# A graph-network layer on one core: selected columns in two of five groups, raw input rows for the first four groups, a later store of the node features

## The chip, the cores and the metric

The kernel runs on one core of a Trainium2 chip. The metric is device time in microseconds (us) of one execution; the time before is the median of three. A core has TensorE (PE; its weight loads are PEld), VectorE (DVE), ScalarE (ACT), GpSimd (POOL) and SyncE (SP, which here only issues transfers), and 16 DMA engines that all queues share. SBUF is the memory the engines work in, PSUM the one that TensorE writes to.

## The reference, cut to what matters

There are 12500 nodes with 64 features and 412500 edges, sorted by receiver (`dst`), each with 32 features.

```python
h = jnp.maximum(_layernorm(x, axis=-1), 0.0)
msg_in = concat([h[src], h[dst], edge_attr_32])         # 64 + 64 + 32
messages = swish(msg_in @ W1 + b1) @ W2 + b2
att = softmax(swish(msg_in @ Wa1 + ba1) @ Wa2 + ba2, axis=0)   # over all edges
aggregated = segment_sum(messages * att, dst)
out = x + swish(concat([h, aggregated]) @ Wu1 + bu1) @ Wu2 + bu2
```

## The kernel before, in words

`[h[src], h[dst], e] @ [Wa1, W1]` is a sum of three terms, and the first two depend on a node alone. So the kernel first makes two tables of 128 columns with a row for each node: `ts_d` (as sender) and `tr_d` (as receiver, with the biases).

**Node stage** (`gnn_kernel`, L164 to L312). x is read in eight chunks (L174, SyncE). For each chunk VectorE and ScalarE normalize: a sum (L219), the mean subtracted (L221), Square (L227), a sum (L232), Sqrt (L235), reciprocal (L240), ReLU and product (L242). TensorE transposes (L254), and ScalarE copies the result into `hT` (L256), which stays in SBUF as 128 x 6272: two nodes' 64 features above each other. From `hT` TensorE makes the rows of `ts_d` (L269, copied at L271, stored at L273) and of `tr_d` (L305, L307, stored at L309 from ScalarE's queue). Then `hT` itself is stored to `hT_d` (L312, same queue). Only `general`, a second way through that runs when the edges' order doesn't suit the first, reads `hT_d`.

**Edge stage** (`one_pass`). Edges are taken in 413 groups of 8 x 125. In iteration g of the main loop (L735) these are issued, each engine keeping the written order (`pin`):

- `begin(g)` (L567): VectorE adds the group's PSUM sum `pe` to its gathered rows `gs` (L570); ScalarE takes Tanh (L573; swish is computed from it).
- pieces of `sum_up` for earlier groups (L711): the softmax weights, TensorE's sum by receiver (L637, L643), the projection (L654), and the addition into `sums` (L668, L672).
- for g < 4 ScalarE fills a quarter of `sums` and of `stand` (L749).
- `burst(g, 0)`, then `load(g + 2)`, `numbers(g + 7)`, `places(g + 6)`, `end(g)`, `burst(g, 1)`.

`load(g)` (L523) takes one of seven `gs` buffers (L161). GpSimd issues the indirect gathers, one for each 125 edges, out of `ts_d` (L530). SyncE loads the edge features `eo` (L541) and receiver numbers `dbs` (L544) for four groups at a time and two windows of `tr_d` (`wins`, L551). VectorE compares (L555), and TensorE adds receiver and edge terms in `pe` (L559). GpSimd runs ahead of the other engines as far as `gs` buffers are free. `end(g)` (L575) reads `gs` for the last time in L583 and L589 on VectorE; L591 and L594 follow.

**Chosen groups** gather 7 times for 8. The last 125 rows are computed instead: SyncE loads their sender numbers (`numbers`, L477), six small VectorE instructions turn them into places in `hT` (`places`, L486 to L492), ScalarE loads the places into registers and copies 125 single columns of `hT` (`columns`, L503) in lots spread over three earlier iterations (`burst`, `SLOTS`), VectorE masks the half that isn't meant (L564), and TensorE multiplies with the stacked weights into `pe` (L565). `begin` then has a copy (L572) for the eighth. Before the change, every third group from 8 to 400 is chosen, 131 of them, in six lots of at most 24 columns.

`load(0)` and `load(1)` stand ahead of the loop, behind the setup of `one_pass` (L420 to L469 on VectorE), whose tiles lie where the node stage's were.

The last part (L799 on) turns `sums` into the output; its length does not depend on the change.

Of the kernel before, what the change touches and what calls it, by code (L numbers as in the profile page):

```python
# [44 lines left out]
F32 = mybir.dt.float32  # L45
I32 = mybir.dt.int32
AF = mybir.ActivationFunctionType
ALU = mybir.AluOpType
AX = mybir.AxisListType
# [4 lines left out]
P = 128  # L54
EP = 125
D = 64
DE = 32
U = 64
C = 2 * U
S1 = U + 1  # L60
K = 8
# [5 lines left out]
H = K // 2  # L67
# [3 lines left out]
NC = 8  # L71
TABLES = 4

EVERY = 3
PHASE = 1
SLOTS = (((0, 24), (24, 24)), ((48, 24), (72, 12)), ((84, 24), (108, 17)))
ROUND = 12582912.0
EPS = 1e-5
NEG = -3.0e38
BIG = 3.0e38  # L80
# [9 lines left out]
def gnn_kernel(ctx: ExitStack, tc: tile.TileContext, n_edges, x, src, src_row, dst, dst_row, first, edge,  # L90
               weights, out):
    nc = tc.nc
    NB = x.shape[0] // P
    T = src.shape[1]
    NG = T // K
# [4 lines left out]
    const = ctx.enter_context(tc.tile_pool(name="const", bufs=1))  # L100
# [4 lines left out]
    hT_d = dram.tile([2 * D, NB // 2, P], F32, name="hT_d")  # L105
# [6 lines left out]
    ident = const.tile([P, P], F32, name="ident")  # L112
# [9 lines left out]
    w_pair = part["pair"].rearrange("p (r n) -> p r n", r=2)  # L122
    wu2h = part["wu2h"].rearrange("p (h d) -> p h d", h=2)
    we, bias, wa2, bu2_r, ba2_c = (part[k] for k in ("we", "bias", "wa2", "bu2", "ba2"))
# [30 lines left out]
    hT = const.tile([2 * D, NB // 2, P], F32, name="hT")  # L155
# [5 lines left out]
    gather = ctx.enter_context(tc.tile_pool(name="gather", bufs=7))  # L161


    with tc.tile_pool(name="node1", bufs=1) as node1, \  # L164
            tc.tile_pool(name="node", bufs=2) as node, \
            tc.tile_pool(name="node_ps", bufs=2, space=PSUM) as node_ps:
# [36 lines left out]
            pin(nc.vector.tensor_tensor(fall, base_p[:, :NG - 1], base_p[:, 1:], ALU.subtract))  # L203
            pin(nc.vector.tensor_reduce(far[:, 2:3], fall, AX.X, ALU.max))

        eps = node1.tile([P, 1], F32, name="eps")
        nc.vector.memset(eps, EPS)
        pin(nc.scalar.activation(node1.tile([P, 1], F32, name="spare"), eps, AF.Sqrt))
        xms, sqs, rstds, hs, tss = ({} for _ in range(5))
# [99 lines left out]
            pin(nc.scalar.dma_start(  # L309
                tr_d[:NP, :].rearrange("(p b) f -> p b f", b=NB)[:, c:c + nn, :], tr))  # L310
        pin(nc.scalar.dma_start(tr_d[NP:, :], zero[:WR, :]))
        pin(nc.scalar.dma_start(hT_d, hT))  # L312

    one_pass(tc, n_edges, locals())
    again = nc.values_load(wrong[0:1, 0:1], min_val=0, max_val=1,
# [77 lines left out]
def one_pass(tc, n_edges, v):  # L393
    nc = tc.nc
# [16 lines left out]
    with ExitStack() as ctx:  # L411
# [43 lines left out]
        with tc.tile_pool(name="work2", bufs=2) as work2, \  # L455
# [12 lines left out]
            for h in range(2):  # L468
                nc.vector.tensor_copy(w2u[:, h, :], w2u_ps)  # L469

            chosen = {g for g in range(8, NG - 12) if g % EVERY == PHASE}

            def numbers(g):
                if g in chosen:
                    e = (g * K + K - 1) * EP
                    n = nums[g] = small.tile([P, EP], I32, name="num", bufs=2)
                    nc.sync.dma_start(n, bass.AP(tensor=v["src_row"].tensor,  # L477
                                                 offset=v["src_row"][:, e:].offset, ap=[[0, P], [1, EP]]))

            def places(g):  # L480
                if g not in chosen:
                    return
                n = nums[g]
                near = small.tile([1, EP], F32, name="near", bufs=1)
                to = small.tile([1, EP], I32, name="to", bufs=2)
                pin(nc.vector.tensor_scalar(to, n[0:1], 1, None, op0=ALU.logical_shift_right))  # L486
                m = NB // 2
                pin(nc.vector.tensor_scalar(near, to, 1.0 / m, 0.5 / m - 0.5, op0=ALU.mult, op1=ALU.add))
                pin(nc.vector.tensor_scalar(near, near, ROUND, None, op0=ALU.add))
                pin(nc.vector.tensor_scalar(near, near, ROUND, float(1 - m * P), op0=ALU.subtract, op1=ALU.mult))  # L490
                pin(nc.vector.scalar_tensor_tensor(to, to, float(P), near, op0=ALU.mult, op1=ALU.add))
                pin(nc.vector.tensor_scalar(n, n, 1, None, op0=ALU.bitwise_and))  # L492
                cols[g] = small.tile([P, EP], F32, name="cols", bufs=2), to

            def columns(g, first, n):
                if g not in chosen:
                    return
                to, at = cols[g]
                _, regs = nc.values_load_multi_w_load_instructions(
                    at[0:1, first:first + n], engines=[ENG.Activation], min_val=0, max_val=NP // 2 - 1,  # L500
                    skip_runtime_bounds_check_because=WHY)
                for i in range(n):
                    pin(nc.scalar.copy(to[:, first + i:first + i + 1], hT[:, bass.ds(regs[i], 1)]))  # L503

            def burst(g, k):
                for i in range(EVERY):
                    columns(g + 3 + i, *SLOTS[EVERY - 1 - i][k])

            at_sp, at_lo, at_hi, bus, rest = {}, {}, {}, {}, {}

# [4 lines left out]
            def registers(g, engine, at, base=base_sb, top=NP - 1):  # L515
# [4 lines left out]
                for i in range(n):  # L520
                    at[g + i] = regs[i]

            def load(g):  # L523

                t = g * K
                if g % NQ == 0:
                    registers(g, ENG.SP, at_sp)
                gs = gss[g] = gather.tile([P, K, C], F32, name="gs")[:EP]
                for j in range(K - (g in chosen)):
                    nc.gpsimd.indirect_dma_start(  # L530
                        out=gs[:, j, :], out_offset=None, in_=ts_d[:, :],
                        in_offset=bass.IndirectOffsetOnAxis(ap=src_sb[:, t + j:t + j + 1], axis=0))
                if g % NQ == 0:
                    n = min(NQ, NG - g) * E2
                    eo = eos[g // NQ % 2]
                    i = g // NQ % 2
                    db = dbs[i * WR:(i + 1) * WR].bitcast(I32)
                    for i in range(g, min(g + NQ, NG)):
                        e = slice((i - g) * E2, (i - g + 1) * E2)
                        ees[i] = eo[:, e], db[:, e]  # L540
                    nc.sync.dma_start(eo[WR:, :n],  # L541
                                      edge[:, g * E2:g * E2 + n])
                    for r in range(2):
                        nc.sync.dma_start(  # L544
                            db[r * R:(r + 1) * R, :n],
                            bass.AP(tensor=dst_row.tensor, offset=dst_row[r:r + 1, g * E2:].offset,
                                    ap=[[0, R], [1, n]]))
                eo, db = ees.pop(g)
                win = wins[g % WINS]
                for r in range(2):  # L550
                    nc.sync.dma_start(win[r * R:(r + 1) * R, :, r, :],  # L551
                                      tr_w[bass.ds(at_sp[g], R), :, :])
                for h in range(2):
                    e = slice(h * E2 // 2, (h + 1) * E2 // 2)
                    pin(nc.vector.tensor_scalar(eo[:WR, e], db[:, e], bj[g // NQ % 2 * WR:(g // NQ % 2 + 1) * WR, g, h:h + 1], None,  # L555
                                                op0=ALU.is_equal))
                pe = pes[g] = pre_ps.tile([P, K, C], F32, name="pe")[:EP]
                for q in range(H):
                    pin(nc.tensor.matmul(pe[:, 2 * q:2 * q + 2, :], eo[:, q * EP:(q + 1) * EP],  # L559
                                         win[:, q // 2, :, :], start=True,  # L560
                                         stop=q < H - 1 or g not in chosen))
                if g in chosen:
                    to, _ = cols[g]
                    pin(nc.vector.scalar_tensor_tensor(to, nums[g], half, to, op0=ALU.is_equal, op1=ALU.mult))  # L564
                    pin(nc.tensor.matmul(pe[:, K - 1, :], to, stack, start=False, stop=True))  # L565

            def begin(g):  # L567

                n = K - (g in chosen)
                pin(nc.vector.tensor_tensor(gss[g][:, :n, :], pes[g][:, :n, :], gss[g][:, :n, :], ALU.add))  # L570
                if n < K:
                    pin(nc.vector.tensor_copy(gss[g][:, n, :], pes[g][:, n, :]))  # L572
                pin(nc.scalar.activation(pes[g], gss[g], AF.Tanh))  # L573
# [111 lines left out]
            def inputs(t):  # L685

                n = P // 2 * NC
                if t < 8:
                    i = (t // 4 + (NG - 1) // NQ + 1) % 2
                    bs[t], xs[t] = eos[i][:, t % 4 * n:(t % 4 + 1) * n], hT[:, t * n:(t + 1) * n]  # L690
                else:
                    gs = gather.tile([P, K, C], F32, name="gs").rearrange("p k c -> p (k c)")
                    bs[t], xs[t] = gs[:, :n], gs[:, n:]
                m = width(t)
                bs[t], xs[t] = bs[t][:, :P // 2 * m], xs[t][:, :m * D]
                nc.sync.dma_start(bs[t], bq_d[t, :, :P // 2 * m])
                nc.sync.dma_start(xs[t], xb_d[t, :, :m * D])
# [37 lines left out]
            for g in range(NG):  # L735
# [38 lines left out]
                        weigh_upto(batch[g])  # L774
                for t in {NG - 5: [0, 1], NG - 4: [2, 3], NG - 2: range(4, NT)}.get(g, []):
                    inputs(t)
                if g == min(30, NG):
                    pin(nc.vector.tensor_reduce(far[:, 0:1], dloc, AX.X, ALU.max))
                    pin(nc.vector.tensor_scalar(far[:, 0:1], far[:, 0:1], -float(R - 1), None,
                                                op0=ALU.add))  # L780
# [357 lines left out]
```

## Time and profile before

| | |
|---|---|
| median of 3 runs | 4922.53 us (4922.45 to 4923.75) |
| the profiled execution | 4935.06 us, span 4933.3 us |
| mean granted TensorE clock | 0.611 |
| gathers (L530) | 3173, of 125 rows of 512 B |
| column copies (L503) | 16375 |
| traffic | HBM read 361.41 MB, written 25.72 MB; 78 GB/s over the span |
| GpSimd's queue | 206.77 MB, 19.0% of the 16 DMA engines |
| the store `hT_d<-hT` | 1 transfer of 3136.0 KB |

The profiled execution takes slightly longer than the others, and the durations below are from it. A busy share is of the whole span. A group of instructions has its line, engine, operation, output and inputs, and count, then its busy time and the mean of one, then the idle time of its engine just ahead of it and what ended it; "issue" means that nothing the profile shows was waited for. A timeline line has start, duration, engine and line; in brackets stands the idle time ahead of it. A transfer's line on a queue is the issue, not its landing.

### The profile page before, as it was taken

Reading aid. Unit: us, or ns where it says so; the run is one execution under the profiler, and the core shown is the slowest. Engines: PE = TensorE matmul, PEld = TensorE weight load, DVE = VectorE, ACT = ScalarE, POOL = GpSimd, SP = SyncE. Lnnn points to the kernel's source line nnn. Section 1 sums busy time; section 2 is a strip of 40 time slices with the busy share of each in tenths; the row PEclk is TensorE's granted clock in tenths of the full one; section 3 lists DMA queues with packets and bytes.
Section 4 is the critical chain, followed back from the end, with each engine's and each line's share of the span. In section 5 each row is a group of like instructions: output and inputs, shape, how many; then the busy total and the mean of one; then the engine's idle time right before and its main releaser. Section 6 shows DMA issues by size and latency. Waiting matters only on the chain. (4 is left out here: it accounts for less than half of the span.)

```text
span 4933.3 us, 81829 instructions
## 1 busy us (share of the span) xinstructions
PE 2429.9 (49%) x11509; PEld 1950.7 (40%) x11509; DVE 3456.5 (70%) x9793; ACT 2214.0 (45%) x17625; POOL 3871.1 (78%) x3198
## 2 busy tenths in 40 slices
PE   5455555445544444544444544444445445444455
PEld 4343344334433333433333443333334334334344
DVE  6677777777776766766766776766767667667667
ACT  3444444444444444444444444444444444444412
POOL 4777877777777777777777777777777777777775
PEclk8666655665666665555665555566566666655655
DMA  7333333333333333333333333233333333333333
GB/s 248 76 76 83 87 75 82 89 74 83 81 75 76 71 74 76 70 75 76 69 76 76 68 76 76 68 76 76 69 76 71 74 76 70 75 76 70 75 91 81
DMA packets 377225, 396.20 MB, mean 80 GB/s; under 512 B 230333, under 2 KB 306039, under 8 KB 376290
## 3 DMA queue, kind: packets, MB, share of 16 engines
q0 software_dynamic: 253840, 206.77, 19.0%
q1 hardware_dynamic: 121458, 174.49, 14.9%
q10 hardware_dynamic: 1376, 9.67, 0.5%
q14 instruction: 457, 3.74, 0.3%
q8 instruction: 94, 1.54, 0.1%
HBM read 361.41 MB, written 25.72 MB: 78 GB/s over the span
## 5 line engine op out<-in xcount | busy, mean ns | idle before, releaser
L530 POOL DMA_INDIRECT gs<-ts_d,src_sb x3173 | 3853.9, 1215 | 1020.6 <-issue 962.4
L559 PE MATMUL pe<-wins,eo 128*125 128x256 f32 x3304 | 1524.4, 637 | 1551.2 <-DVE eo L555 1288.7
L503 ACT COPY cols<-hT 128x1 f32 x16375 | 1630.2, 189 | 754.3 <-issue 749.8
L559 PEld LDWEIGHTS pe<-wins,eo 128*125 128x125 f32 x3304 | 997.4, 319 | 1872.4 <-DVE eo L555 1375.5
L570 DVE TENSOR_TENSOR gs<-pe,gs 125x1024 f32<-125x1024 f32 (+1 forms) x413 | 487.5, 1180 | 1153.1 <-DMA gs<-ts_d,src_sb 1140.2
L573 ACT ACTIVATE pe<-gs 125x1024 f32<-125x1024 f32 x413 | 424.8, 1029 | 1768.2 <-DVE gs L570 859.2
L637 DVE TENSOR_SCALAR wt<-iota_w,dloc,p 125x40 f32<-125x40 f32 x3304 | 772.5, 364 | 1.8
L643 PE MATMUL sp<-wt,acts 125*65 125x40 f32 x6608 | 652.2, 270 | 13.2 <-DVE wt L637 9.2
L643 PEld LDWEIGHTS sp<-wt,acts 125*65 125x65 f32 x6608 | 612.5, 185 | 23.6 <-DVE wt L637 14.0
L613 PE MATMUL mt<-ident,mx 125*128 125x125 f32 x110 | 48.1, 438 | 644.7 <-DVE sums L672 608.1
L654 PEld LDWEIGHTS mt<-ss,w2u 65*128 65x128 f32 x826 | 210.7, 283 | 362.0 <-issue 235.4
L654 PE MATMUL mt<-ss,w2u 65*128 65x40 f32 x826 | 188.3, 322 | 262.8 <-DVE gm L620 199.4
L555 DVE TENSOR_SCALAR eo<-dbs,bj 64x250 f32<-64x250 int32 x826 | 303.2, 397 | 17.9 <-DMA dbs<-in_dst_row_dram 8.5
L591 DVE TENSOR_TENSOR pe<-pe,w_all 125x512 f32<-125x512 f32 x413 | 288.8, 699 | 13.7
L589 DVE SCALAR_TENSOR_TENSOR pe<-pe,gs 125x512 f32<-125x512 f32 x413 | 287.4, 696 | 10.8
L583 DVE SCALAR_TENSOR_TENSOR acts<-pe,gs 125x512 f32<-125x512 f32 x413 | 284.6, 689 | 12.8 <-issue 2.4
L594 DVE TENSOR_REDUCE lg<-pe 125x8 f32<-125x512 f32 x413 | 284.2, 688 | 10.8
L613 PEld LDWEIGHTS mt<-ident,mx 125*128 125x128 f32 x110 | 20.0, 182 | 655.8 <-issue 652.2
L675 DVE COPY stand<-nmax 64x40 f32 x826 | 217.1, 263 | 3.3
L672 DVE TENSOR_TENSOR sums<-sums,mt 64x40 f32 x606 | 114.4, 189 | 4.7 <-issue 0.4
L668 DVE SCALAR_TENSOR_TENSOR sums<-sums,scale,mt 64x40 f32 x220 | 55.8, 254 | 78.4 <-PE mt L654 59.6
L356 DVE TENSOR_SCALAR bu<-mt,w_all 64x256 f32<-64x256 f32 (+1 forms) x50 | 23.9, 478 | 92.6 <-PE mt L347 78.6
(124 smaller groups left out, 1123.2 us busy)
## 6 DMA issues: line engine op xcount, KB each, us to landing
eo<-in_edge_dram SPq DMA_DIRECT2D x103, 500.0 KB
dbs<-in_dst_row_dram SPq DMA_DIRECT2D x206, 250.0 KB
gs<-ts_d,src_sb POOLq DMA_INDIRECT x3173
wins<-tr_d SPq DMA_DIRECT2D x826, 32.0 KB
num<-in_src_row_dram SPq DMA_DIRECT2D x131, 62.5 KB
ts_d<-ts SPq DMA_DIRECT2D x5, 896.0 KB
tr_d<-tr ACTq DMA_DIRECT2D x5, 896.0 KB
hT_d<-hT ACTq DMA_DIRECT2D x1, 3136.0 KB
```

Of the source, the lines that this page charges most:

```text
L503: pin(nc.scalar.copy(to[:, first + i:first + i + 1], hT[:, bass.ds(regs[i], 1)]))
L530: nc.gpsimd.indirect_dma_start(out=gs[:, j, :], out_offset=None, in_=ts_d[:, :], in_offset=bass.IndirectOffsetOnAxis(ap=src_sb[:, t + j:t ...
L555: pin(nc.vector.tensor_scalar(eo[:WR, e], db[:, e], bj[g // NQ % 2 * WR:(g // NQ % 2 + 1) * WR, g, h:h + 1], None, op0=ALU.is_equal))
L559: pin(nc.tensor.matmul(pe[:, 2 * q:2 * q + 2, :], eo[:, q * EP:(q + 1) * EP], win[:, q // 2, :, :], start=True, stop=q < H - 1 or g not in ...
L570: pin(nc.vector.tensor_tensor(gss[g][:, :n, :], pes[g][:, :n, :], gss[g][:, :n, :], ALU.add))
L573: pin(nc.scalar.activation(pes[g], gss[g], AF.Tanh))
L583: pin(nc.vector.scalar_tensor_tensor(acts[g % ACTS][:, :, 0:U], th[:, :, U:C], 1.0, gs[:, :, U:C], op0=ALU.add, op1=ALU.mult))
L589: pin(nc.vector.scalar_tensor_tensor(att, th[:, :, 0:U], 1.0, gs[:, :, 0:U], op0=ALU.add, op1=ALU.mult))
L591: pin(nc.vector.tensor_tensor(att, att, wa2[:EP, None, :].to_broadcast([EP, K, U]), ALU.mult))
L637: pin(nc.vector.tensor_scalar(wt[:, j, :], iota_w[:EP, j // H, :], dloc[:, g * K + j:g * K + j + 1], p[:, k + j:k + j + 1], op0=ALU.is_equ ...
L643: pin(nc.tensor.matmul(sp, acts[g % ACTS][:, j, :], wt[:, j, :], start=j == 0, stop=j == K - 1))
L654: pin(nc.tensor.matmul(pp, w2u.rearrange("s h u -> s (h u)"), sps.pop(g), start=True, stop=True))
```

## The change

- **Columns.** Chosen are groups whose number modulo 5 is 1 or 4, again from 8 to 400. A group's 125 columns come in five lots (four of 24, one of 29), so that each iteration's two bursts have one lot each. The tiles `num`, `to` and `cols` get three buffers for two.
- **First four groups.** At the kernel's start, four `gs` buffers are filled by 32 gathers out of the input x itself (rows of 64 numbers), whose indices have a small load of their own. In place of the gathers out of `ts_d`, `load(g)` for g < 4 calls `features(g)`: it normalizes the rows on the edges (VectorE and ScalarE), transposes them (TensorE) and copies them back (ScalarE); a second product in `load` adds the sender's term to `pe`, and `begin` copies `pe` instead of adding.
- **Store of hT.** The one store from ScalarE's queue at the end of the node stage becomes seven from SyncE's, in iterations 20 to 26.

```diff
-EVERY = 3
-PHASE = 1
-SLOTS = (((0, 24), (24, 24)), ((48, 24), (72, 12)), ((84, 24), (108, 17)))
+LOTS = ((0, 24), (24, 24), (48, 24), (72, 24), (96, EP - 96))
+ROUNDS = 5
+SLOTS = {1: ((5, 1), (4, 0), (4, 1), (3, 0), (3, 1)), 4: ((5, 0), (5, 1), (4, 0), (4, 1), (3, 0))}
+RAW = 4
...
     gather = ctx.enter_context(tc.tile_pool(name="gather", bufs=7))
+    raw_src = const.tile([P, RAW * K], I32, name="raw_src")
+    nc.scalar.dma_start(raw_src, src[:, :RAW * K])
+    raws = [gather.tile([P, K, C], F32, name="gs") for _ in range(RAW)]
+    for g in range(RAW):
+        for j in range(K):
+            nc.gpsimd.indirect_dma_start(
+                out=raws[g].rearrange("p k c -> p (k c)")[:EP, j * D:(j + 1) * D], out_offset=None, in_=x[:, :],
+                in_offset=bass.IndirectOffsetOnAxis(ap=raw_src[:EP, g * K + j:g * K + j + 1], axis=0))
...
-        pin(nc.scalar.dma_start(hT_d, hT))
...
-            chosen = {g for g in range(8, NG - 12) if g % EVERY == PHASE}
+            chosen = {g for g in range(8, NG - 12) if g % ROUNDS in SLOTS}
...
             def burst(g, k):
-                for i in range(EVERY):
-                    columns(g + 3 + i, *SLOTS[EVERY - 1 - i][k])
+                for i in (3, 4, 5):
+                    slots = SLOTS.get((g + i) % ROUNDS, ())
+                    if (i, k) in slots:
+                        columns(g + i, *LOTS[slots.index((i, k))])
...
+            def features(g):
+                gs = gss[g] = v["raws"][g][:EP]
+                xg, xm = (gs[:, h * H:(h + 1) * H, :].rearrange("p k (r d) -> p (k r) d", d=D) for h in range(2))
+                total = small.tile([EP, K], F32, name="raw_t", bufs=1)
+                pin(nc.vector.tensor_reduce(total, xg, AX.X, ALU.add))
+                pin(nc.vector.scalar_tensor_tensor(xm, total[:, :, None].to_broadcast([EP, K, D]), -1.0 / D, xg,
+                                                   op0=ALU.mult, op1=ALU.add))
+                pin(nc.scalar.activation(xg, xm, AF.Square))
+                rstd = small.tile([EP, K], F32, name="raw_r", bufs=1)
+                pin(nc.vector.tensor_reduce(rstd, xg, AX.X, ALU.add))
+                pin(nc.scalar.activation(rstd, rstd, AF.Sqrt, bias=v["eps"][:EP], scale=1.0 / D))
+                pin(nc.vector.reciprocal(rstd, rstd))
+                pin(nc.vector.scalar_tensor_tensor(xg, xm, 0.0, rstd[:, :, None].to_broadcast([EP, K, D]),
+                                                   op0=ALU.max, op1=ALU.mult))
+                pt = one_ps.tile([P, 4, P], F32, name="mt")[:, :, :EP]
+                for q in range(H):
+                    pin(nc.tensor.transpose(pt[:, q, :], xg[:, 2 * q:2 * q + 2, :], ident[:EP, :EP]))
+                to = raw_to[g] = v["raws"][g][:, H:, :EP]
+                pin(nc.scalar.copy(to, pt))
...
-                gs = gss[g] = gather.tile([P, K, C], F32, name="gs")[:EP]
-                for j in range(K - (g in chosen)):
+                if g < RAW:
+                    features(g)
+                else:
+                    gss[g] = gather.tile([P, K, C], F32, name="gs")[:EP]
+                gs = gss[g]
+                for j in range(0 if g < RAW else K - (g in chosen)):
...
                     pin(nc.tensor.matmul(pe[:, 2 * q:2 * q + 2, :], eo[:, q * EP:(q + 1) * EP],
                                          win[:, q // 2, :, :], start=True,
-                                         stop=q < H - 1 or g not in chosen))
+                                         stop=g >= RAW and (q < H - 1 or g not in chosen)))
+                    if g < RAW:
+                        pin(nc.tensor.matmul(pe[:, 2 * q:2 * q + 2, :], raw_to[g][:, q, :], v["w_pair"][:, 0],
+                                             start=False, stop=True))
...
-                pin(nc.vector.tensor_tensor(gss[g][:, :n, :], pes[g][:, :n, :], gss[g][:, :n, :], ALU.add))
+                if g < RAW:
+                    pin(nc.vector.tensor_copy(gss[g], pes[g]))
+                else:
+                    pin(nc.vector.tensor_tensor(gss[g][:, :n, :], pes[g][:, :n, :], gss[g][:, :n, :], ALU.add))
...
+                if 20 <= g < 27:
+                    n = -(-(NB // 2) // 7)
+                    q = slice((g - 20) * n, min((g - 19) * n, NB // 2))
+                    nc.sync.dma_start(v["hT_d"][:, q, :], v["hT"][:, q, :])
```

More of the change, by code (lines that the diff above doesn't have):

```diff
@@ L204, in windows @@
             pin(nc.vector.tensor_reduce(far[:, 2:3], fall, AX.X, ALU.max))
-        eps = node1.tile([P, 1], F32, name="eps")
+        eps = const.tile([P, 1], F32, name="eps")
         nc.vector.memset(eps, EPS)
@@ L475, in numbers @@
                     e = (g * K + K - 1) * EP
-                    n = nums[g] = small.tile([P, EP], I32, name="num", bufs=2)
+                    n = nums[g] = small.tile([P, EP], I32, name="num", bufs=3)
                     nc.sync.dma_start(n, bass.AP(tensor=v["src_row"].tensor,
@@ L484, in places @@
                 near = small.tile([1, EP], F32, name="near", bufs=1)
-                to = small.tile([1, EP], I32, name="to", bufs=2)
+                to = small.tile([1, EP], I32, name="to", bufs=3)
                 pin(nc.vector.tensor_scalar(to, n[0:1], 1, None, op0=ALU.logical_shift_right))
@@ L492, in places @@
                 pin(nc.vector.tensor_scalar(n, n, 1, None, op0=ALU.bitwise_and))
-                cols[g] = small.tile([P, EP], F32, name="cols", bufs=2), to
+                cols[g] = small.tile([P, EP], F32, name="cols", bufs=3), to
             def columns(g, first, n):
@@ L521, in registers @@
                     at[g + i] = regs[i]
+            def features(g):
[17 more added lines that the diff above has]
+                pin(nc.scalar.copy(to, pt))
+            raw_to = {}
             def load(g):
```

## The prediction

> **What bounds the kernel now.** I read the busy table and the costliest groups first, then GpSimd's own timeline from end to end, then the other engines around its first gathers, and last one iteration of the loop.
>
> The groups of the page (line, engine, operation, count; then busy us, mean ns; then idle time ahead and what ended it):
>
> ```profile
> PE 2429.9 (49%) x11509; PEld 1950.7 (40%) x11509; DVE 3456.5 (70%) x9793; ACT 2214.0 (45%) x17625; POOL 3871.1 (78%) x3198
> ...
> L530 POOL DMA_INDIRECT gs<-ts_d,src_sb x3173 | 3853.9, 1215 | 1020.6 <-issue 962.4
> ...
> L503 ACT COPY cols<-hT 128x1 f32 x16375 | 1630.2, 189 | 754.3 <-issue 749.8
> L570 DVE TENSOR_TENSOR gs<-pe,gs 125x1024 f32<-125x1024 f32 (+1 forms) x413 | 487.5, 1180 | 1153.1 <-DMA gs<-ts_d,src_sb 1140.2
> L573 ACT ACTIVATE pe<-gs 125x1024 f32<-125x1024 f32 x413 | 424.8, 1029 | 1768.2 <-DVE gs L570 859.2
> ```
>
> GpSimd (POOL) does nothing but 3173 gathers, and its idle time is "issue": it waits for no one. VectorE (DVE) waits 1140.2 us for gathers, 2.76 us in each of 413 groups, and ScalarE (ACT) waits for VectorE. GpSimd's timeline shows where the row starts and how it runs:
>
> ```profile
> 51.89 1.38 POOL L530 DMA_INDIRECT gs<-ts_d,src_sb  x1 [49.48 <-issue]
> 53.57 1.21 POOL L530 DMA_INDIRECT gs<-ts_d,src_sb  x1 [0.31 <-issue]
> ...
> 140.77 1.21 POOL L530 DMA_INDIRECT gs<-ts_d,src_sb  x1 [0.30 <-issue]
> ...
> 152.90 1.21 POOL L530 DMA_INDIRECT gs<-ts_d,src_sb  x1 [0.30 <-issue]
> ```
>
> Before 51.89 GpSimd is empty for 49.48 us, because the gathered table ts_d must be stored first. Group 7's first gather (the 57th) starts at 140.77, group 8's (the 65th) at 152.90, the last at 4875.68. From group 8 to the last are 3108 steps: 4722.8 / 3108 = **1.5196 us a gather**, with no gap worth naming. The end behind the last gather, some 57 us, is not touched by the change. So two things count: how many gathers there are from group 8 on, and when group 8's first one starts.
>
> **Part 1: columns.** Chosen groups are those from 8 to 400: with one in three 131, with two in five 78 + 79 = 157. Each saves a gather: 26 x 1.5196 = **39.5 us**. What it adds lies on engines that wait:
> - ScalarE: 26 x 125 = 3250 column copies. The first row below gives 24 in 2.32 us, 0.097 each: 315 us, 0.8 us for each of 393 groups. Register loads stay (785 lots of columns for 786). Waits before the tanh hide it (3.76 us in the second row).
> - VectorE: L486 to L492 take 1.75 us, L564 0.35, L572 0.28: 2.38 x 26 = 62 us, 0.16 a group, hidden in its 2.76. Without cover it would cost those 62.
> - TensorE: 52 more passes at L565 of 376 ns, 20 us, at 49% busy. SyncE: 26 loads of 62.5 KB; its own waits are for TensorE at L551, so nothing queues behind them that is late.
>
> ```profile
> 1014.16 2.32 ACT L503 COPY cols<-hT 128x1 f32 x24 [1.49 <-issue]
> ...
> 1020.65 1.03 ACT L573 ACTIVATE pe<-gs 125x1024 f32<-125x1024 f32 x1 [3.76 <-DVE gs L570]
> ```
>
> One row speaks against it. The gather that starts at 122.44, beside L486 to L490, took 1.33 us for 1.21:
>
> ```profile
> 122.44 1.33 POOL L530 DMA_INDIRECT gs<-ts_d,src_sb  x1 [0.30 <-issue]
> ```
>
> All that the 3173 gathers take beyond 1.21 (those over 1.22) sums to 9.9 us; laid wholly on 131 chosen groups it is 0.075 each, 2 us for 26. I take 0, range 0 to 2 (fewer gathers than now can't lock it less than not at all). The Trainium skill's page "SBUF — State Buffer", section "Who interferes with whom", says that VectorE's copy and tensor_scalar can take two ports and then block GpSimd for the whole instruction. By that rule the five tensor_scalar of `places` (1.46 us) could cost 26 x 1.46 = 38 us and leave almost nothing of this part; the trace shows a twentieth of it.
>
> **Part 2: the first four groups.** Their 32 gathers go to the front, where GpSimd was empty. Their indices are a small load like the first x chunk's, which VectorE used at 3.72; 32 x 1.52 from there ends at 52.3. A 256 B row may cost half (27.8) or as much as the slowest early one (1.38 + 0.30: 57.5); neither matters below. Their DMA work, at the queue's 19.0% x 4933 / 3173 = 0.295 us of all 16 engines each, is 9.5 us at most, and the engines are 71% busy in the first 52 us, so the node stage slips by 0 to 9.5. A full stretch (74 to 85) gave this queue 8.0%, so about 1 us in the full ten (10 to 20); I take **1**. Then groups 4, 5, 6: 24 gathers from 52.9 end at **89.4**.
>
> Now a new wait: there are seven buffers, four hold raw rows, so group 7 waits for the end of group 0's work, and everything on GpSimd waits behind it. When is that? Before, it stood thus:
>
> ```profile
> 74.05 1.12 ACTq L312 DMA_DIRECT2D hT_d<-hT  x1
> 77.09 0.59 SPq L541 DMA_DIRECT2D eo<-in_edge_dram  x1
> ...
> 87.98 1.21 POOL L530 DMA_INDIRECT gs<-ts_d,src_sb  x1 [1.19 <-DMA gs<-ts_d,src_sb]
> 91.82 1.21 POOL L530 DMA_INDIRECT gs<-ts_d,src_sb  x1 [2.63 <-DMA gs<-ts_d,src_sb]
> ...
> 92.93 1.12 DVE L555 TENSOR_SCALAR eo<-dbs,bj 64x250 f32<-64x250 int32 x4 [8.55 <-DMA dbs<-in_dst_row_dram]
> ...
> 94.45 7.40 PE L559 MATMUL pe<-wins,eo 128*125 128x256 f32 x24 [23.84 <-DMA wins<-tr_d]
> ...
> 98.23 1.22 DVE L570 TENSOR_TENSOR gs<-pe,gs 125x1024 f32<-125x1024 f32 x1 [4.18 <-PE pe L559]
> ...
> 99.52 1.28 ACT L573 ACT_TABLE_LOAD   x1 [51.29 <-DMA eo<-in_edge_dram]
> ```
>
> The 3136 KB store of hT lies ahead of the loads that group 0 needs. With it gone, 1.0 MB of eo and dbs at 272 GB/s takes some 4 us from 77.7, and wins, issued at 82.2, is there by about 86. That no longer is last. What is late next is `features`, behind VectorE's setup, which ends at 84.4:
> - features(0): two reduces and two of L589's kind on 512 elements (0.69 each), Square 0.63, Sqrt 0.30, reciprocal 0.2, some 0.1 per change of engine: 4.4. Four transposes 1.1 (L254), the copy 0.6 (L256) and changes: 6.3 after the start, 90.7.
> - the sum in TensorE is now 16 passes for 8: 7.5 by 94.45 to 98.2 (8 in 3.75), 4.9 by 24 in 7.40. I take 7.5, as the clock is at 0.5 there: 98.3.
> - begin(0) on VectorE at 98.3; `tensor_copy` lies between L572's 0.28 and L570's 1.18, I take 1.1. Behind it stands features(2) before group 0's two instructions that free the buffer. Tanh and its table load are done 3.6 after begin, the two fills (L749) at 6.5, Square 7.15, reduce 7.95, a table load of 1.28 and Sqrt 9.6, reciprocal and product 10.6, eo 11.2, message and weight (L583, L589) **12.6**; before this was 5.1 (98.23 to 103.3).
>
> So buffer 0 is free at 98.3 + 12.6 + 1 = **111.9**. Group 1 follows with 1.45 (L591, L594) and the same 12.6 (features(3), two table loads): **126.0**. Group 2 has no features behind it: 5.1 + 1.45, 132.6. GpSimd: group 7 from 112.0, done at 124.2, waits, group 8 at **126.1**, done at 138.3, and group 9's buffer is long free. Group 8 is 152.9 - 126.1 = **26.8 us** earlier than before. Of the 48.5 us of gathers moved, plus what the hT store cost, about 25 are given back as this wait.
>
> If features start at 77.2, with VectorE's setup behind them, buffer 0 is free 7 earlier; if the node stage slips by 9.5, 8.5 later: gain 18 to 34.
>
> Table loads: the row at 99.52 has 1.28, and the tanh starts at 100.81 behind it. The skill's page "ScalarE: Activation LUTs", section "What ACT_TABLE_LOAD costs", adds a drain of 1.38 us to each switch; by it the three new switches ahead of 126.1 would cost 4.1 us more. The trace shows no such gap.
>
> **Part 3: store of hT.** Seven issues of 448 KB on SyncE at 0.42 (L697's price), in groups 20 to 26, where the DMA engines are a third busy: 1.6 us each, ahead of window loads that are issued two groups early. I take 0; without cover 7 x 1.6 = 11, and a gain is excluded, as the bytes are the same and only moved out of part 2's stretch, where they are counted.
>
> **The sum.** 39.5 + 26.8 = 66.3 off the profiled 4935.06 (span 4933.3 and 1.8 around it): 4868.8. The median without profile, 4922.53, is 12.5 lower; the same difference gives **4856**. Own range 4849 (gain 34) to 4867 (gain 18, the port's 2).
>
> **Rivals.**
> - *Nothing waits* (0.12): features finish by 89 and group 8 starts at 52.9 + 32 x 1.52 = 101.5; gain 51.4 + 39.5: **4832**. For it: raw rows land early. Against: the features stand in VectorE's order behind setup and begin(0).
> - *The early start is lost* (0.14): contention in the node stage, a later buffer 1 at 152 instead of 126: only the columns count, **4883**.
> - *The port blocks GpSimd* (0.04): 38 of the 39.5 are eaten: **4895**; with the case before as well (0.03), **4921**, no change.
> - *ScalarE becomes the bound* (0.05), slower. In the iteration from 1008.62 its work ends after 8.28 us, 4.66 of them 48 columns; so 3.62 + 50 columns. GpSimd's iteration falls to 7.6 x 1.5196 = 11.55; with the early gain spread out, ScalarE makes the kernel slower from 11.72 on, 0.162 us a column. At the unoverlapped 189 ns it is 13.07, 1.42 x 393 - 27 = +531: **5454**. For it: ScalarE's order holds the tanh behind the columns. Against: 0.097 measured.
>
> **Chances.** Forecast 0.62, rivals as given. Faster by over 0.2% (what a measurement here can tell): 0.62 + 0.12 + 0.14 + 0.04 = 0.92; within 0.03; slower 0.05. The range 4830 to 4885 holds the forecast, *nothing waits* and *early start lost*, 0.88.
>
> **What would show it.** 3091 gathers from the table behind group 7's start, still 1.52 apart; a GpSimd gap of some 23 us near 89 that ends with group 0, and a short one near 124; tanh still waiting for VectorE, now about 3 us. Wrong if the gathers' step grows, if ScalarE's idle time at L573 is gone, or if group 8 starts outside 118 to 135.

## The result, and the profile after

The changed kernel takes **4863.53 us** (median; 4860.96 to 4864.56) beside 4922.49 of the kernel before (4922.34 to 4923.75): ratio 0.9879, interval 0.9862 to 0.9896, 59.0 us less. The profiled execution took 4863.94 us, span 4862.2. It is a typical one, where that of before was 12.5 above its median (the kernel before takes 4922.5 us in some executions and some 10 us more in others), so profiles differ by 71.1 us and medians by 59.0.

The page's groups after (same columns as before):

```profile
PE 2447.0 (50%) x11609; PEld 1966.1 (40%) x11609; DVE 3519.7 (72%) x10021; ACT 2514.4 (52%) x20891; POOL 3838.3 (79%) x3172
L568 POOL DMA_INDIRECT gs<-ts_d,src_sb x3115 | 3775.1, 1212 | 972.1 <-issue 893.4
L512 ACT COPY cols<-hT 128x1 f32 x19625 | 1925.2, 187 | 959.4 <-issue 936.9
L614 DVE TENSOR_TENSOR gs<-pe,gs 125x1024 f32<-125x1024 f32 (+1 forms) x409 | 478.9, 1171 | 1012.5 <-DMA gs<-ts_d,src_sb 1001.0
L617 ACT ACTIVATE pe<-gs 125x1024 f32<-125x1024 f32 x413 | 424.2, 1027 | 1227.4 <-DVE gs L614 661.6
```

GpSimd's idle time is still mostly "issue", VectorE still waits for gathers, and the 3250 more column copies came out of ScalarE's wait ahead of the tanh (L617): 1227.4 us for 1768.2. Now the start, where the next two fences are the timeline's rows from 45 to 60 and from 60 to 119:

```profile
45.06 3.59 DVE L203 TENSOR_TENSOR dloc<-dst_sb,base_p 125x3304 f32<-125x3304 int32 x1
45.15 4.91 POOL L170 DMA_INDIRECT gs<-in_x_dram,raw_src  x1 [0.30 <-issue]
52.21 8.13 SPq L824 DMA_DIRECT2D hT_d<-hT  x7
59.55 1.21 POOL L568 DMA_INDIRECT gs<-ts_d,src_sb  x1 [0.30 <-issue]
```

```profile
70.78 2.22 DVE L317 TENSOR_TENSOR tr<-pn,w_all 128x512 f32<-128x512 f32 x4 [4.54 <-DMA tr_d<-tr]
88.38 0.40 DVE L429 MEMSET bases<- 1x414 int32 x1 [4.44 <-issue]
94.53 1.28 POOL L568 DMA_INDIRECT gs<-ts_d,src_sb  x1 [0.30 <-issue]
106.27 1.22 DVE L612 COPY gs<-pe 125x1024 f32<-125x1024 f32 x1 [2.17 <-PE pe L601]
118.42 1.21 POOL L568 DMA_INDIRECT gs<-ts_d,src_sb  x1 [22.61 <-DVE pe L635]
```

Read them in order. The 32 early gathers (L170) run from 3.79 to 59.55, one of them held for 4.91 us beside VectorE's L203. Then **all seven stores of hT are issued between 52.2 and 60.3**, not in iterations 20 to 26. In the first row of the second fence VectorE waits 4.54 us for a `tr_d` store to land. The node stage ends, and `one_pass` begins with L429, at 88.38; before it was at 77.24. The 24 gathers of groups 4 to 6 are followed by a gap of 22.61 us, which ends with group 0's last instructions (`end`, L635), as buffer 0 comes free: group 7 starts at 118.42. Group 8 starts at 130.53, with no second gap: 22.4 us earlier than before. From there to the last gather (4805.20) are 3082 steps of 1.5168 us; before it was 3108 of 1.5196. The stretch behind the last gather is 57.0 us.

### The profile page after: what moved, and what is told of

It reads as the page before. It is cut to its first block, busy times and chain, and to the rows that moved or that the text cites. A ratio compares the mean times of both kernels' runs of the same rounds, so it can differ in the third digit from the quotient of the medians.

```text
span 4862.2 us, 88819 instructions
## 1 busy us (share of the span) xinstructions
PE 2447.0 (50%) x11609; PEld 1966.1 (40%) x11609; DVE 3519.7 (72%) x10021; ACT 2514.4 (52%) x20891; POOL 3838.3 (79%) x3172
## 5 line engine op out<-in xcount | busy, mean ns | idle before, releaser
L568 POOL DMA_INDIRECT gs<-ts_d,src_sb x3115 | 3775.1, 1212 | 972.1 <-issue 893.4
L512 ACT COPY cols<-hT 128x1 f32 x19625 | 1925.2, 187 | 959.4 <-issue 936.9
L617 ACT ACTIVATE pe<-gs 125x1024 f32<-125x1024 f32 x413 | 424.2, 1027 | 1227.4 <-DVE gs L614 661.6
L635 DVE TENSOR_TENSOR pe<-pe,w_all 125x512 f32<-125x512 f32 x413 | 288.7, 699 | 13.8
L633 DVE SCALAR_TENSOR_TENSOR pe<-pe,gs 125x512 f32<-125x512 f32 x413 | 287.2, 695 | 10.7
L627 DVE SCALAR_TENSOR_TENSOR acts<-pe,gs 125x512 f32<-125x512 f32 x413 | 283.8, 687 | 10.7 <-ACT pe L617 1.4
L606 PEld LDWEIGHTS pe<-stack,cols 128*125 128x125 f32 x314 | 92.7, 295 | 25.6
```

What stands on the lines that cost most here:

```text
L568: nc.gpsimd.indirect_dma_start(out=gs[:, j, :], out_offset=None, in_=ts_d[:, :], in_offset=bass.IndirectOffsetOnAxis(ap=src_sb[:, t + j:t ...
L633: pin(nc.vector.scalar_tensor_tensor(att, th[:, :, 0:U], 1.0, gs[:, :, 0:U], op0=ALU.add, op1=ALU.mult))
L635: pin(nc.vector.tensor_tensor(att, att, wa2[:EP, None, :].to_broadcast([EP, K, U]), ALU.mult))
```

## The experiments

The experiments ran on three chips, called A, B and C here: those with fixed columns and *third_raw* on B, *end_first* on C, all others on A. Which chip the recorded pair ran on isn't on record; the median of the kernel before is 4922.5 us there, 4923.5 on C, and 4932 to 4934 on A and B. Every ratio is against the kernel before, run beside it on the same chip. Starts of gathers and ends of the node stage are from profiles; on A those of the kernel before are from *before_again* (node stage 76.09, group 8 at 151.12) and those of the changed kernel from *after_again* (86.88 and 128.79), both 1 to 2 us earlier than in the recorded pair.

**The start.** Theory: the stores of hT, early, took the DMA time of `tr_d`'s stores. Rival: the early gathers made the node stage late.

*store_late* pins the seven stores, on ScalarE's queue, to the place in the loop where they are written:

```diff
-                    nc.sync.dma_start(v["hT_d"][:, q, :], v["hT"][:, q, :])
+                    pin(nc.scalar.dma_start(v["hT_d"][:, q, :], v["hT"][:, q, :]))
```

> The changed kernel with the seven stores on ScalarE's queue in its written order, so that they are issued in iterations 20 to 26 for certain. Theory: the node stage ends near 80 instead of 88, buffer 0 is free near 111 instead of 118, group 8 starts near 123 instead of 130.5: 7.5 us faster than the changed kernel, 4856. Rival (the raw gathers hold up the node stage): it still ends near 88, and the time stays within 2 us of the changed kernel's 4863.5.

The stores are issued from 345 to 415. The node stage's end, and the first gathers of groups 7 and 8:

```profile
78.33 0.40 DVE L429 MEMSET bases<- 1x414 int32 x1 [4.21 <-DMA tr_d<-tr]
108.04 1.21 POOL L568 DMA_INDIRECT gs<-ts_d,src_sb  x1 [12.84 <-DVE pe L635]
120.17 1.21 POOL L568 DMA_INDIRECT gs<-ts_d,src_sb  x1 [0.30 <-issue]
```

Against the changed kernel on the same chip the node stage ends 8.6 us earlier (78.33 for 86.88), and so does group 8's start (120.17 for 128.79). So the early stores cost the start 8.6 us, and the rival falls. But the time was 4979.41: ratio 1.0098 (1.0083 to 1.0114), since the steps behind group 8 had grown to 1.549.

*raw_only* leaves columns at one in three and hT's store at its old place:

```diff
...
+        pin(nc.scalar.dma_start(hT_d, hT))
...
-                for i in (3, 4, 5):
...
+                for i in range(EVERY):
+                    columns(g + 3 + i, *SLOTS[EVERY - 1 - i][k])
...
-                if 20 <= g < 27:
...
-                    nc.sync.dma_start(v["hT_d"][:, q, :], v["hT"][:, q, :])
```

> The first four groups from raw rows alone; columns as before, the one store of hT where it was, at the end of the node stage. Theory (the node stage ended 11 us late in the changed kernel because the seven stores were issued beside the table's stores; the raw gathers cost it only 2 to 3 us): the node stage ends near 80 instead of 88, group 0's buffer comes free near 115, group 8's first gather starts near 127, 25 us off, 4897. Rival (the raw gathers themselves make the node stage late): it ends near 88 here as well, and the hT store then comes on top, so group 8 starts at 135 or later, 18 us off or less, 4905.

Node stage ended at 78.40, group 7 at 115.31, group 8 at 127.41; ratio 0.9962 (0.9948 to 0.9976), 19.1 us less. The start gains 23.7 us against *before_again* (151.12 - 127.41), with the one long store still ahead of group 0's loads: group 8 is 7 later than in *store_late*. The early gathers cost the node stage 2.3 us (78.40 for 76.09); the forecast took 1.

*store_only* is the kernel before with nothing but the seven stores from SyncE in place of the one:

```diff
-        pin(nc.scalar.dma_start(hT_d, hT))
...
+                if 20 <= g < 27:
...
+                    nc.sync.dma_start(v["hT_d"][:, q, :], v["hT"][:, q, :])
```

> The kernel before with the move of the hT store alone. Theory (the seven stores are not held back to iterations 20 to 26, as nothing that they need comes late): they are issued at about 45 to 60 us, beside the stores of tr_d, the node stage ends some 8 us later than 77, but GpSimd's row starts at 51.9 as before and waits for no buffer, so the time stays within 5 us of before. Rival (they are issued in iterations 20 to 26): issues between 300 and 400 us, the node stage ends at 77, group 0's sum starts some 8 us earlier, and GpSimd's waits at 88 and 92 are gone, 3 us off.

The stores are issued from 47.69 on here too, the node stage ended at 83.33, and group 8 started at 148.31; ratio 0.9994 (0.9985 to 1.0003). So with nothing else changed the node stage ends 7.2 us later, but group 8 starts 2.8 us earlier than in *before_again*: there three gathers near 90 us, beside the one long store, wait 3.8 us together for earlier gathers to land, and here none does. In all there is no measurable difference. Up to group 8 GpSimd's row waits for no buffer in either, so a late node stage costs it nothing. The store's cost in the change is one against a late store.

*early_features* keeps the stores late and normalizes the four groups' rows between the steps of the `tr_d` loop (`next(steps)` behind each), not in `load`:

> The changed kernel with the hT stores on ScalarE's queue in iterations 20 to 26 and with the features of the first four groups computed between the last steps of the node stage, where VectorE waits for stores of tr_d. Theory (GpSimd's 23 us wait for buffer 0 is this chain): that wait shrinks to some 4 us, group 8 starts near 110 instead of 130.5; where ScalarE's copies run through, 20 us faster than the changed kernel, 4844. Rival (the wait is set by the window and edge loads): group 8 starts within 5 us of store_late's 120. Where the copies are broken up, ScalarE sets the pace and the time shows nothing of it.

Both theories missed. The node stage ended at 96.22, since the added work stands in VectorE's and TensorE's order ahead of the sums that `tr_d`'s stores wait for. Group 8 started at 127.44, 7 later than in *store_late*; 4974.15 us, ratio 1.0074 (1.0031 to 1.0116).

**The columns.** *cols_only* is the kernel before with two groups in five and the new lots, nothing else:

```diff
-EVERY = 3
...
+ROUNDS = 5
+SLOTS = {1: ((5, 1), (4, 0), (4, 1), (3, 0), (3, 1)), 4: ((5, 0), (5, 1), (4, 0), (4, 1), (3, 0))}
...
```

> The kernel before with the columns in two of five groups alone; 26 gathers fewer. Theory (GpSimd's row of gathers sets the time, the added work lies beside waits): 26 x 1.52 = 39.5 us off, 4883, the step between gathers unchanged at 1.517 to 1.520, ScalarE still waiting some 3 us ahead of each tanh. Rival (the columns give back part on ScalarE or by locking GpSimd, and the early start gave more than the trace says): less than 30 us off, above 4892.

It took 4994.88: ratio 1.0119 (1.0103 to 1.0134), slower instead of faster. Steps from group 8 on are 1.559 us, 73 of them over 2 us. Two of these long steps, from its timeline (L575, L585 and L591 are L617, L627 and L633 after: the tanh and the two instructions of `end` that read the gathered rows):

```profile
600.61 0.69 DVE L585 SCALAR_TENSOR_TENSOR acts<-pe,gs 125x512 f32<-125x512 f32 x1 [5.20 <-ACT pe L575]
601.34 0.70 DVE L591 SCALAR_TENSOR_TENSOR pe<-pe,gs 125x512 f32<-125x512 f32 x1
602.91 1.21 POOL L532 DMA_INDIRECT gs<-ts_d,src_sb  x1 [3.52 <-issue]
618.04 0.70 DVE L591 SCALAR_TENSOR_TENSOR pe<-pe,gs 125x512 f32<-125x512 f32 x1
619.60 1.21 POOL L532 DMA_INDIRECT gs<-ts_d,src_sb  x1 [4.89 <-issue]
```

The profile calls GpSimd's idle time "issue", but both gathers start 0.86 us behind the end of an L591, the last reading of a `gs` buffer. That is so for 71 of the 73 long steps, and in *after_again* below for 74 of 76: GpSimd waits for a buffer. And ahead of the first of them VectorE had waited 5.20 us for the tanh. Is it the columns, or the chip? The changed kernel itself was run there, the same file, with the kernel before and *cols_only* once more:

> The changed kernel once more, to be read beside the columns alone in the same group of runs. In the first four experiments ScalarE's column copies came in runs of 5 to 6 with 0.4 us between them (15 to 18 in the profiles of before and after), and the two kernels with 50 columns a group were bound by that. Theory C (it belongs to the chip that the runs came to, not to the kernels): on a chip where the copies are broken up, this kernel is slow too, near 4970 to 4990, and above before; on a chip where they run through, it is near 4864. Theory K (it belongs to the kernels, by where their instructions lie): this one is near 4864 whatever the columns alone do beside it.

> The kernel before, for its profile on the same chip. Theory C: its column copies come in the same lengths as those of the kernels beside it (runs of 5 if they are slow, of 15 if not). Theory K: runs of 15 in any case.

> The columns in two of five groups alone, once more. Theory C: near 4990 with copies in short runs if the changed kernel beside it is slow, and 39 us under before if it is not. Theory K: near 4990 again, with the changed kernel beside it fast.

*after_again* took 4982.85, ratio **1.0085 (1.0044 to 1.0126)**: on this chip the change makes the kernel slower. *cols_again*: 5010.23, ratio 1.013 (1.0092 to 1.0168). *before_again*: 4959.89 in one run, where the kernel before took 4932.18 to 4963.60 in this series. ScalarE's rows show what is different. First the changed kernel in the recorded profile, then the same kernel on chip A (timeline of ScalarE, near 1020):

```profile
1024.49 2.32 ACT L512 COPY cols<-hT 128x1 f32 x24 [0.65 <-issue]
1028.31 2.32 ACT L512 COPY cols<-hT 128x1 f32 x24 [1.50 <-issue]
```

```profile
1027.59 0.28 ACT L512 COPY cols<-hT 128x1 f32 x2 [0.56 <-issue]
1028.36 0.28 ACT L512 COPY cols<-hT 128x1 f32 x2 [0.49 <-issue]
1029.12 0.38 ACT L512 COPY cols<-hT 128x1 f32 x3 [0.47 <-issue]
1029.91 0.28 ACT L512 COPY cols<-hT 128x1 f32 x2 [0.41 <-issue]
```

On the one, a lot of 24 runs through. On the other, two or three copies come, then a gap, again every 0.75 us or so. Over the stretch from 600 to 4600 us the copies came in runs of 17.8 on average on the first and 6.2 on the second; all eight profiles on chip A have runs of 4.9 to 6.3, all four others with register-given columns 14.8 to 18.1. What that leaves of the waits is in the groups for that stretch, ScalarE's copies and tanh, then VectorE's first instruction of `begin` and its first behind the tanh, each with the idle time ahead of it; the recorded profile first:

```profile
L512 ACT COPY cols<-hT 128x1 f32 x17332 | 1700.4, 187 | 848.8 <-issue 829.4 <-DVE sums L712 4.5 <-DVE fall L667 4.4
L617 ACT ACTIVATE pe<-gs 125x1024 f32<-125x1024 f32 x347 | 356.5, 1027 | 1008.8 <-DVE gs L614 502.6 <-DVE gs L616 260.8 <-DMA gs<-ts_d,src_sb 244.1
L614 DVE TENSOR_TENSOR gs<-pe,gs 125x1024 f32<-125x1024 f32 (+1 forms) x347 | 405.6, 1169 | 926.2 <-DMA gs<-ts_d,src_sb 916.7 <-issue 8.0
L627 DVE SCALAR_TENSOR_TENSOR acts<-pe,gs 125x512 f32<-125x512 f32 x346 | 237.8, 687 | 8.1
```

```profile
L512 ACT COPY cols<-hT 128x1 f32 x16831 | 1854.1, 187 | 1584.1 <-issue 1492.2 <-DVE wt L681 36.0 <-DVE eo L593 24.9
L617 ACT ACTIVATE pe<-gs 125x1024 f32<-125x1024 f32 x337 | 346.0, 1027 | 142.3 <-DMA gs<-ts_d,src_sb 70.3 <-issue 39.5 <-DVE wt L681 9.7
L614 DVE TENSOR_TENSOR gs<-pe,gs 125x1024 f32<-125x1024 f32 (+1 forms) x337 | 393.2, 1167 | 29.5 <-DMA gs<-ts_d,src_sb 11.5 <-issue 8.6
L627 DVE SCALAR_TENSOR_TENSOR acts<-pe,gs 125x512 f32<-125x512 f32 x338 | 233.5, 691 | 559.8 <-issue 379.1 <-ACT pe L617 176.3
```

Busy time and gaps of the copies fill 2549 of the 4000 us on the first, 0.147 us a column, and 3438 on the second, 0.204. One copy takes the same 187 ns on both; the gaps differ. The tanh waits 2.9 us there and 0.4 here. VectorE's waits have changed places: there it waits 926.2 us for gathers and 8.1 for the tanh, here 29.5 and 559.8. So on chip A the gathers come early enough, and it is ScalarE that sets the pace: its tanh comes late, `end` comes late, the buffer comes late, and GpSimd has 76 steps over 2 us, 1.5607 a step on average (in the profiled execution, of 5007.38 us). These rows speak against a rival that no experiment tested on that chip, that GpSimd or its transfers are slower there. The kernel before is near the same edge there: in *before_again* VectorE waits 29.6 us for gathers and 351.0 for the tanh, at 1.522 a step. With the other engines behind, the stretch after the last gather is longer too, 65.6 to 76.0 us in the profiles on A.

**Why are the copies broken up?** Theory: the registers, since each copy's column number is loaded. Rival: the chip gives ScalarE its instructions more slowly, whatever they are. The two kernels with fixed columns leave out the register loads and with them the choice of the right column:

```diff
-    pin(nc.scalar.copy(to[:, first + i:first + i + 1], hT[:, bass.ds(regs[i], 1)]))
+    pin(nc.scalar.copy(to[:, first + i:first + i + 1], hT[:, (first + i) * 32:(first + i) * 32 + 1]))
```

> The changed kernel with as many column copies, but of fixed columns: the places are still computed, but ScalarE neither loads them into registers nor works out an address before each copy. What it leaves out is the choice of the right column. Theory S (on this chip ScalarE's supply of column instructions is what binds): tanh waits 3 us again, GpSimd's step is back at 1.517, group 8 to the last takes 3082 x 1.517, so about 128 + 4675 + 59 = 4862, some 110 us under the changed kernel here. Rival G (GpSimd or its transfers are slower on this chip, and ScalarE only waits along): the step stays near 1.555, 4975.

> The kernel before with fixed columns, which leaves out the choice of the right column. Theory S: the 41.7 columns a group lie at the edge of what ScalarE can take here, so the gain is only what this chip adds to the kernel before, about 10 us: 4923. With the changed kernel's fixed columns beside it this gives what the change is worth where ScalarE costs nothing: about 61 us. Rival G: no change, 4933.

They ran on chip B, where *third_raw* shows the register form in long runs (14.8), so they can't tell theory and rival apart: **that stays open**. With fixed columns the copies' group has no idle time at all in *before_fixed* (666.6 us with registers in *third_raw*, which has as many columns; 600 to 4600), so the register-given form costs ScalarE its gaps on that chip. And they measure the change with ScalarE relieved: *before_fixed* took 4932.25, ratio 1.0 (0.9991 to 1.001); *after_fixed* 4870.55, ratio 0.9873 (0.9857 to 0.989), 61.7 less than *before_fixed*. Group 8 starts at 130.32 for 151.98, which is 21.7 of it; the other 40.0 are left for the 26 gathers, 1.54 each. The forecast of 4923 for *before_fixed* was for a chip like A, and can't be tested here.

**A better start.** In the first two iterations `load(g + 2)`, with its `features`, stands ahead of the `end(g)` that frees the buffer. *third_raw* and *end_first* turn that round, with the stores of hT late as in *store_late*; *third_raw* has one column group in three, *end_first* two in five:

```diff
+                if g < RAW - AHEAD:
+                    end(g)
                 if g + AHEAD < NG:
                     load(g + AHEAD)
...
-                end(g)
+                if g >= RAW - AHEAD:
+                    end(g)
```

> Columns in one of three groups as before; the first four groups from raw rows; the hT stores on ScalarE's queue in iterations 20 to 26; and in the first two iterations the end of the group goes ahead of the load that calls features. Theory: the two instructions that free buffer 0 no longer stand behind features(2), so group 7 starts near 102 instead of store_late's 108, group 8 near 114 instead of 120; 39 us under before on any chip, 4894 here. Rival (on this chip ScalarE at 41.7 columns has nothing left and gives the early start back): less than 15 us, above 4918.

*third_raw*: 4894.67, ratio 0.9923 (0.9906 to 0.9939), 37.6 less; group 8 at 115.08, 36.9 earlier than in *before_fixed* on the same chip. What the start gains arrives at the end in full.

> The changed kernel (columns in two of five, raw rows for four groups) with the hT stores on ScalarE's queue in iterations 20 to 26 and, in the first two iterations, the end of the group ahead of the load that calls features. Theory, on a chip where ScalarE's copies run through: group 8 starts at 115 as in third_raw instead of 130.5, 15 us off the changed kernel, 77 under before in the same group of runs (4855 beside 4932, 4846 beside 4922); tanh still waits some 3 us. On a chip where the copies are broken up: the start is as early, but ScalarE's tanh waits for nothing, GpSimd's step is near 1.55 and the time near 4970, above before. Rival (the early start is given back in the steady part on any chip): within 5 us of the changed kernel.

*end_first*: **4849.35** (4848.11 to 4850.73), ratio **0.9850 (0.9834 to 0.9867)**, 74.2 less than before on that chip, and faster than both kernels of the recorded pair. GpSimd's timeline, group 6's last gather, then groups 7 and 8:

```profile
95.18 1.21 POOL L568 DMA_INDIRECT gs<-ts_d,src_sb  x1 [0.30 <-issue]
102.36 1.21 POOL L568 DMA_INDIRECT gs<-ts_d,src_sb  x1 [5.97 <-DVE pe L635]
...
114.86 1.21 POOL L568 DMA_INDIRECT gs<-ts_d,src_sb  x1 [0.30 <-issue]
```

The wait of 22.61 us has shrunk to 5.97. Steps stay at 1.5167, and the tanh still waits 2.9 us. *end_first* and *third_raw* differ in the columns alone, though on two chips: their gains differ by 74.2 - 37.6 = 36.6 us, beside 39.5 forecast for the columns.

## Why the prediction was right, and where it was not

**Right: what sets the time, and the columns.** 66.3 us were forecast and 59.0 measured (ratio interval: 51 to 68). As forecast, GpSimd's row sets the time, and what counts is the number of gathers and the start of group 8. *Columns*: 26 gathers fewer at the measured step are 26 x 1.517 = 39.4, forecast 39.5. The two recorded profiles differ by 48.1 from group 8 to the last gather, because the step also fell from 1.5196 to 1.5168, 8.7 over 3100 of them; that isn't put down to the change, since *before_fixed*, profiled in an execution of 4922.51 us, has 1.5159, and *after_fixed* 1.5200. With 39.4 and the start's 22.4 the sum is 61.8, 2.8 more than the medians show; where these went isn't shown. Tanh waits were forecast at "about 3 us" and are 2.9; the added copies were hidden here. *TensorE, VectorE, SyncE*: no step of theirs shows in GpSimd's row. *The port*: all that the 3115 gathers take beyond 1.21 us (those over 1.22, as counted before) sums to 9.5 us, for 157 chosen groups 0.061 each, against 0.075 before. So the five small `tensor_scalar` still don't lock GpSimd for their length.

**Wrong: part 3, "in groups 20 to 26" and "I take 0".** The step assumed that a transfer is issued where its line stands. Line 824 is not pinned, and of the loop's work it needs nothing but `hT`, so SyncE issued it right behind `ts_d`'s last store, beside the first two of the eight `tr_d` stores. The same 3136 KB were not "moved out of part 2's stretch": they were moved from its end towards its start. The node stage ended at 88.38 instead of the forecast 78.2. On chip A, where both were run, the early place cost 8.6 us in GpSimd's row (128.79 for 120.17). *store_late* changes the queue as well as the pinning, so it shows what the early issue costs, not which of the two holds a store back.

**Also undersized: the early gathers.** They took 55.8 us for 48.6, 3.7 of it in the one beside L203, and held up the node stage by 2.3 (*raw_only*) where part 2 took 1.

**Luck: the chain from the node stage to buffer 0.** That `features` stands last ahead of group 0's sum was right, but its pieces were put too long. From the node stage's end to the free buffer the forecast has 77.2 to 110.9, 33.7 us; it took 30.0 (88.38 to 118.42): VectorE's setup 6.6 for 7.2, features and the sum for group 0 11.3 for 13.9, begin to free 12.15 for 12.6. And the second wait, where group 1 was to free its buffer 2 us after it was needed, didn't come. So a node stage 10.2 us later than forecast met a chain some 5.7 shorter, and group 8 came 4.4 late, at 130.53 for 126.1. Buffer 0's wait, forecast at "some 23 us", is 22.61 only because both of its ends moved alike: it runs from 95.8 to 118.4, forecast 89.4 to 112.0. The later gathers of groups 4 to 6 cost nothing, since the wait ends with group 0.

**The rival that got 0.05 happens on chip A.** *ScalarE becomes the bound* had the kernel slower "from 11.72 on, 0.162 us a column", and against it "0.097 measured". The mechanism and its place were right: in *after_again* the iteration is 7.6 x 1.5607 = 11.86 us, just past 11.72, and the kernel is slower than before. Its price was far off (+531 forecast, +48.9 measured). The copies' pitch went to 0.204 with gaps, even above the 0.189 of that price; but 50 x 0.204 = 10.2 leaves only 1.7 of the 11.86 for all else, where the rival added 3.62. Its 3.62 held the gaps ahead of the lots, which the 0.204 holds already. What was wrong is the argument against it: 0.097 us a column was read in one profile of one chip, and the same copies have another pitch on chip A. There the columns alone are a loss (1.0119 and 1.013 in two series), and the start alone is a gain (0.9962).

**Shown and not shown.** Shown: what the early stores cost (one chip, one edit); that in the same kernel ScalarE has slack in one profile and none in the other, with the copies broken up in the second; that the long steps on A end with a buffer, and the buffer with a late tanh. Only argued: that without the breaks A's steps would be short (no run there took them away). Open: why the copies are broken up, and whether it is that chip's for good; two series of runs there agree. The mean granted TensorE clock on A was 0.586 to 0.605, elsewhere 0.607 to 0.620; no run separates that.

## What to carry to other kernels

A transfer that is written later is not issued later unless something holds it there: look up its issue in the trace, and ask of every moved transfer what it depends on. When work is moved into an engine's slack, take the engine's time per iteration, gaps included, and ask what it would be at the slowest pitch seen: where that reaches the bound, measure on more than one chip. And where buffers are handed to early work, the wait moves to the instruction that frees the first one, so that instruction should stand ahead of work that is not yet needed.

## What the runs showed of the hardware

- The pace of small copies at register-given columns differs between profiles of the same kernel: lots of 24 run through in 2.32 us in the recorded profile, and come in runs of two to six with gaps of 0.3 to 0.6 us on chip A.
- An indirect gather on GpSimd can be held up by one VectorE instruction: 4.91 us for 1.21, beside L203 (3.59 us, both inputs in SBUF). The Trainium skill, page "SBUF — State Buffer", section "Who interferes with whom", says that a VectorE instruction with two SBUF inputs contends with a GpSimd instruction that reads SBUF; this row agrees (the gather's indices lie in SBUF). In all eight profiles with early gathers the one beside L203 took 3.5 to 4.9 us.
- A gather of 256 B rows (L170) costs GpSimd what one of 512 B rows does, 1.21 us in the median and 0.30 to the next: between these two sizes the number of gathers counts, not their bytes.
